# A scan over sixteen states: both channel halves of a state in turn, and five states weighed on another engine

## The chip, the core and the metric

The kernel runs on one core of a Trainium2 chip. A core has five engines with an instruction queue each, worked through in order: TensorE (PE in the profile: matrix products into PSUM, and PEld, its weight loads), VectorE (DVE), ScalarE (ACT), GpSimd (POOL) and SyncE (SP, which here only issues DMA transfers). They wait for each other by semaphores. The metric is the device time of the whole kernel in microseconds; the times shown are those of several executions, and the profile is that of one more.

## What is computed

Four layers over x of shape 2 x 1024 x 128. Each layer normalizes x and adds an attention-like part and a feed-forward part, both of the normalized x. The change lies in layer 2, whose first part is a Mamba block and whose second is a mixture of 14 experts of which each token uses two.

```python
def _L2_attn_ref(x, W_in, conv_w, conv_b, W_x, W_dt, b_dt, A_log, D_param, W_out):
    D_STATE = 16
    D_INNER = 256
    xz = x @ W_in
    xc, z = jnp.split(xz, 2, axis=-1)
    ...
    xc = jax.nn.silu(xc)
    x_dbl = xc @ W_x
    dt_raw = x_dbl[..., :1]
    B_mat = x_dbl[..., 1:1 + D_STATE]
    C_mat = x_dbl[..., 1 + D_STATE:]
    dt = jax.nn.softplus(dt_raw @ W_dt + b_dt)
    A = -jnp.exp(A_log)

    def step(h, inp):
        x_t, dt_t, B_t, C_t = inp
        dA = jnp.exp(dt_t[..., None] * A)
        h = dA * h + dt_t[..., None] * B_t[:, None, :] * x_t[..., None]
        y = jnp.einsum('bds,bs->bd', h, C_t)
        return (h, y)
    ...
    _, ys = lax.scan(step, h0, xs)
    y = jnp.moveaxis(ys, 0, 1) + D_param * xc
    y = y * jax.nn.silu(z)
    return y @ W_out
```

The recurrence runs over 1024 positions for each of 2 batches, 256 channels and 16 states. Every state of a channel is a recurrence of its own; the output of a channel is the sum of its 16 states, each weighed with its row of C.

## The kernel before

`layer2` (L1897) records two generators in turn: `l2_mamba` (L1641), the Mamba block, and the experts (`l2_experts`, `moe_sparse`). Each `yield` of `l2_mamba` hands over; `in_turn` then lets the experts record one piece, at two of three yields up to the 96th yield or so and at every other one behind it. The instructions of both therefore stand interleaved in each engine's queue in the order in which they were recorded, and the loop of the scan lies under `manual_schedule()`, so that nothing is moved afterwards.

The channels lie on the 128 partitions in NH = 2 halves (a), the positions of a batch (b) in two chunks (o) of CH = 512. One scan handles one state s of one half of one chunk: 2 x 2 x 2 x 16 = N = 128 steps k, and `at(k)` (L1767) says which. Before the change the 16 states of one half come first and then the 16 of the other half. What is prepared ahead of the loop: dt and dx = dt * xc for every half, the 16 rows of B written to DRAM (`bd`, L1727) and those of C, split into three bf16 parts, laid into `cst` (L1734).

For each step the loop (L1829 to L1853) records, in this order:

- `inputs(k + 3)` (L1782): GpSimd multiplies dx by the row of B, giving `su`. The row, broadcast to all partitions, was loaded by `load` (L1774) on SP's queue into one of 16 buffers `bb`; the second half uses the rows that the first half loaded.
- `decays(k + 3)` (L1788): ScalarE makes the decays `da` = exp(dt * A) in PSUM, four buffers.
- the `yield`, where a piece of the experts is recorded.
- `scan(k)` (L1794): VectorE's scan over 512 positions, giving `sh`; in the second chunk it starts from `carry`, the last column of the first chunk, which ScalarE copied (L1839).
- the product of step k - 1 (L1843): VectorE weighs `sh` with the row of C, `pc`, giving `spr`. VectorE's order is thus scan k, product k - 1, scan k + 1.
- `rows_c(k)` (L1801): TensorE spreads row s of C over all partitions by a bf16 matmul with a selecting matrix, into the single PSUM bank `pc`, once a step.
- the sum of step k - 1 (L1848): TensorE adds `spr` to the bank `py` by a matmul with the identity (fp32, two passes in the trace), over 16 states.

After 16 states `end` (L1807) adds D * xc on VectorE and multiplies by silu(z) on GpSimd, in place of dx. `project` (L1815) multiplies a finished chunk by W_out, into a bank of `da`; VectorE adds the result to x one step later. PSUM is full: four banks `da`, one `pc`, one `py`, two for the experts.

An expert (`moe_sparse`) records, with a yield between: four transposes m_pt of its rows on TensorE and their copy m_xeT on ScalarE; two products m_ph (two passes each) and their activation m_h on ScalarE, which loads a table for it and another for the next exp; the product m_py and m_yT; four transposes m_pb, the copy m_ye and its store on SP's queue. Its weights m_w and rows m_xe are loaded on SP's queue two experts ahead. When all 14 experts are done, the tokens fetch their rows: GpSimd issues 32 indirect DMAs m_yg (L840); ScalarE and VectorE weigh and add them (m_rows, L857 and L859), TensorE turns four of them back (m_back), and VectorE clips them and adds them to x (m_clip).

The kernel holds all four layers twice: a general branch for inputs that overfill an expert stands behind a flag and doesn't run here.

Of the kernel before, what the change touches and what calls it, by code (L numbers as in the profile page):

```python
# [1640 lines left out]
def l2_mamba(c, w, xnT, xT):  # L1641
# [7 lines left out]
    with ExitStack() as es:  # L1649
# [41 lines left out]
        xc, zs, dt, dx, bd = {}, {}, {}, {}, []  # L1691
        for b in range(B):
# [36 lines left out]
            bd.append(d)  # L1729
            for o in range(0, S, CH):  # L1730
# [27 lines left out]
        bp = es.enter_context(tc.tile_pool(name="s_bp", bufs=16))  # L1758
        wk = es.enter_context(tc.tile_pool(name="s_wk", bufs=3))
        N = 2 * B * NH * L2_DS  # L1760
        carry = {}
# [3 lines left out]
        bb, us, das, hs, pcs, pys = {}, {}, {}, {}, {}, {}  # L1765

        def at(k):  # L1767

            r, s = divmod(k, L2_DS)
            r, a = divmod(r, NH)  # L1770
            b, o = divmod(r, 2)
            return b, o, a, s

        def load(k):  # L1774

            if k < N:
                b, o, a, s = at(k)
                if a == 0:
                    t = bb[2 * b + o, s] = bp.tile([P, CH], F32, tag="bb", name=f"bb{k}")
                    nc.sync.dma_start(t, bd[b][s, o * CH : (o + 1) * CH].partition_broadcast(P))  # L1780

        def inputs(k):  # L1782
            if k < N:
                b, o, a, s = at(k)
                us[k] = wk.tile([P, CH], F32, tag="su", name=f"su{k}")
                nc.gpsimd.tensor_tensor(us[k], dx[b, a][:, o * CH : (o + 1) * CH], bb[2 * b + o, s], ALU.mult)  # L1786

        def decays(k):  # L1788
            if k < N:
                b, o, a, s = at(k)  # L1790
                das[k] = pa.tile([P, CH], F32, tag="da", name=f"da{k}", bufs=4)
                nc.scalar.activation(das[k], dt[b, a][:, o * CH : (o + 1) * CH], AF.Exp, scale=am[:, a, s : s + 1])  # L1792

        def scan(k):  # L1794
            b, o, a, s = at(k)
            hs[k] = wk.tile([P, CH], F32, tag="sh", name=f"sh{k}")
# [4 lines left out]
        def rows_c(k):  # L1801
            if k < N:
                b, o, a, s = at(k)
                pcs[k] = pa.tile([P, CH], F32, tag="pc", name=f"pc{k}")
                mm(c, pcs[k], sel3[:, s, :], cst[b][:, o * CH : (o + 1) * CH])
# [9 lines left out]
        def project(b, o):  # L1815
            po = pa.tile([P, CH], F32, tag="da", name=f"s_po{b}_{o}", bufs=4)
# [3 lines left out]
            return lambda: tt(c, xo, xo, po, ALU.add)  # L1820

        add = None
        with tc.manual_schedule():
            for k in range(L2_DS):
                load(k)
            for k in range(3):
                inputs(k)
                decays(k)
            for k in range(N + 1):  # L1829
                inputs(k + 3)  # L1830
                load(k + 19)
                decays(k + 3)
                if k < N:
                    yield
                    scan(k)
                if k:
                    b, o, a, s = at(k - 1)
                    if o == 0:
# [433 lines left out]
```

## Time and profile before

| what | value |
|---|---|
| three runs | 2029.17, 2033.06, 2038.33 us; median 2033.06 |
| the profiled execution | 2022.65 us, its span 2020.9 |
| busy over the span: PE, DVE, ACT, POOL | 1634.6, 1264.2, 1265.9, 413.6 us |
| the scan loop, 1528 to 1826 us: PE, DVE, ACT, POOL | 234.88, 255.92, 170.25, 202.01 us |
| clock granted to TensorE in these 298 us | 0.89 |
| scan without and with carry, mean | 1217 and 1276 ns, 64 of each |
| da, mean | 690 ns, 128 |

The page of the profile gives the busy time of each engine, the span in 40 slices, the chain of work that ended last, and groups of equal instructions by line and tile with their mean time and the idle time in front of them, put down to what ended it. Where a helper records an operation (`mm` at L51, `tt` at L63), its line is the helper's, and the tile's name tells which it is. Other views give the instructions of a window in order of time, the busy time by window, and who waited for whom. A matmul's duration overlaps its neighbour's, so the distance from start to start is what it costs TensorE.

### The profile page before, as it was taken

How to read it: one execution, taken by the hardware profiler on the slowest of the kernel's cores; microseconds unless marked ns; L12 is line 12 of the kernel's file. 1: busy time of each engine (PE TensorE's matmuls, PEld its weight loads, DVE VectorE, ACT ScalarE, POOL GpSimd, SP SyncE). 2: the span in 40 equal slices, each digit the busy share in tenths (PEclk: the TensorE clock that was granted, in tenths of full speed). 3: DMA queues.
4: the chain of work that ended last, by engine and by line, in shares of the span. 5: the costliest groups of instructions: out<-in, count | busy, mean ns of one | idle time of the engine just before them, and what ended most of it. 6: DMA issues, size and time to landing. Idle time of an engine off the chain costs nothing. (4 is left out here: it accounts for less than half of the span.)

```text
span 2020.9 us, 18408 instructions
## 1 busy us (share of the span) xinstructions
PE 1634.6 (81%) x5978; PEld 730.2 (36%) x5978; DVE 1264.2 (63%) x2130; ACT 1265.9 (63%) x2116; POOL 413.6 (20%) x413
## 2 busy tenths in 40 slices
PE   4699999999688789988888772987785999566784
PEld 2232322222234334433333340654332444223563
DVE  4788866881365446446556338554457998785673
ACT  3378756786477787887877665654556778223451
POOL 2000000000000200000300017033056666761110
PEclk7799989999788899999999885986787999778897
DMA  4521110100100210100100001110014443100000
GB/s 107 161 63 32 25 26 2 25 1 2 48 6 12 62 31 26 31 21 16 38 5 0 8 12 35 58 43 23 9 37 152 136 161 102 42 15 18 6 6 12
DMA packets 76817, 81.66 MB, mean 40 GB/s; under 512 B 12759, under 2 KB 57590, under 8 KB 75560
## 3 DMA queue, kind: packets, MB, share of 16 engines
q1 hardware_dynamic: 67224, 62.68, 10.5%
q0 software_dynamic: 7888, 16.93, 3.4%
q8 instruction: 49, 0.80, 0.2%
q10 hardware_dynamic: 1600, 0.79, 0.2%
q14 instruction: 56, 0.46, 0.1%
HBM read 55.18 MB, written 24.44 MB: 39 GB/s over the span
## 5 line engine op out<-in xcount | busy, mean ns | idle before, releaser
L487 DVE TENSOR_REDUCE maxes<-sc 128x1 f32<-128x1024 f32 x256 | 303.6, 1219 | 79.1 <-PE sc L51 78.3
L602 ACT ACTIVATE ex<-st 128x512 f32<-128x512 f32 x512 | 277.1, 599 | 102.9 <-PE st L51 97.5
L51 PE MATMUL st<-qst,kst 75*128 75x512 bf16 x512 | 178.7, 391 | 8.4 <-DMA qst<-mt 5.6
L51 PE MATMUL sc<-kst,qst 72*128 72x512 bf16 x512 | 161.1, 399 | 28.0 <-DMA kst<-scr 14.1
L1786 POOL TENSOR_TENSOR su<-dx,bb 128x512 f32<-128x512 f32 x128 | 162.3, 1273 | 83.1 <-DVE sh L1797 76.2
L780 POOL DMA_INDIRECT m_x<-m_rows,m_to x80 | 98.6, 1232 | 335.6 <-DVE m_back L742 188.8
L840 POOL DMA_INDIRECT m_yg<-m_y,m_back x80 | 79.8, 998 | 422.9 <-DVE a_y L1045 311.2
L51 PE MATMUL py<-spr,ident 128*128 128x512 f32 x256 | 146.9, 658 | 0.0
L1792 ACT ACTIVATE da<-dt,am 128x512 f32<-128x512 f32 x128 | 87.6, 690 | 83.4 <-DVE sh L1797 79.4
L51 PE MATMUL av<-ex,va 128*9 128x512 f32 x1024 | 139.2, 613 | 0.0
L51 PE MATMUL a_ph<-a_x,wf 128*128 128x512 f32 x256 | 122.6, 614 | 12.7 <-DVE a_x L1046 9.3
L51 PE MATMUL a_pf<-a_h,wf 128*128 128x512 f32 x256 | 114.1, 599 | 0.0
L51 PE MATMUL pc<-cst,sel 80*128 80x512 bf16 x128 | 52.8, 413 | 74.9 <-DVE spr L63 71.0
L51 PEld LDWEIGHTS <-kst 75*128 75x128 bf16 x512 | 49.1, 98 | 168.9 <-issue 126.3
L1007 ACT ACTIVATE a_h<-a_ph,cols 128x512 f32<-128x512 f32 x128 | 84.9, 687 | 33.4 <-PE a_ph L51 33.2
L51 PEld LDWEIGHTS py<-spr,ident 128*128 128x128 f32 x256 | 53.3, 209 | 126.4 <-issue 99.9
L51 PE MATMUL a_pQ<-a_y,wqkvo 128*128 128x512 f32 x56 | 48.0, 1007 | 53.7 <-DVE a_y L1046 53.7
L63 DVE TENSOR_TENSOR spr<-sh,pc 128x512 f32<-128x512 f32 x128 | 85.3, 667 | 8.1 <-PE pc L51 7.9
L63 DVE TENSOR_TENSOR a_r<-a_r,a_x 128x512 f32<-128x512 f32 x32 | 22.0, 690 | 99.1 <-ACT a_r L1018 99.1
L1797 DVE TENSOR_TENSOR_SCAN sh<-da,su 128x512 f32<-128x512 f32 x64 | 77.9, 1217 | 7.5 <-POOL su L1786 4.0
L51 PEld LDWEIGHTS <-qst 72*128 72x128 bf16 x512 | 51.5, 101 | 85.7 <-issue 45.4
L1797 DVE TENSOR_TENSOR_SCAN sh<-da,carry,su 128x512 f32<-128x512 f32 x64 | 81.7, 1276 | 0.2 <-ACT carry L1839 0.2
(541 smaller groups left out, 3224.0 us busy)
## 6 DMA issues: line engine op xcount, KB each, us to landing
bb<-bd SPq DMA_DIRECT2D x64, 256.0 KB
m_w<-in_L_ffn_w_dram SPq DMA_DIRECT2D x44, 128.0 KB
m_xe<-m_x SPq DMA_DIRECT2D x22, 256.0 KB
m_y<-m_ye SPq DMA_DIRECT2D x22, 256.0 KB
qst<-scr POOLq DMA_DIRECT2D x24, 192.0 KB, 9.1
kst<-scr SPq DMA_DIRECT2D x24, 192.0 KB
wf<-in_L_attn_Wf_dram SPq DMA_DIRECT2D x16, 256.0 KB
m_x<-zero SPq DMA_DIRECT2D x1, 3584.0 KB
```

Of the source, the lines that this page charges most:

```text
L51: c.nc.tensor.matmul(out, lhsT, rhs, start=start, stop=stop)
L63: c.nc.vector.tensor_tensor(out, a, b, op)
L487: nc.vector.tensor_reduce(mx[:, t % HT, i : i + 1], sc, AX.X, ALU.max)
L602: nc.scalar.activation(ex, st, AF.Exp)
L780: nc.gpsimd.indirect_dma_start(views[K * t + k][:, :], bass.IndirectOffsetOnAxis(ap=to[:, k, t : t + 1], axis=0), rows[:, t, :], None)
L840: nc.gpsimd.indirect_dma_start(g, None, ys[:, :], bass.IndirectOffsetOnAxis(ap=back[:, k, t : t + 1], axis=0))
L1007: nc.scalar.activation(half(b, f"h{f}", o, "h", f"h{l}_{b}_{f}_{o}", bufs=8), ph, AF.Gelu_apprx_tanh, bias=c.cols["bf1"][:, 4 * l + f : 4 ...
L1786: nc.gpsimd.tensor_tensor(us[k], dx[b, a][:, o * CH : (o + 1) * CH], bb[2 * b + o, s], ALU.mult)
L1792: nc.scalar.activation(das[k], dt[b, a][:, o * CH : (o + 1) * CH], AF.Exp, scale=am[:, a, s : s + 1])
L1797: nc.vector.tensor_tensor_scan(hs[k], das[k], us[k], carry[b, a][:, s : s + 1] if o else 0.0, ALU.mult, ALU.add)
```

## The change

The two halves of a state now follow each other (`at`), so a state is two steps long and both use one load of B and one bank `pc`. Half of the buffers `bb` go; `su` and `sh` get a fourth, `da` drops to three, and each half has a bank `py` of its own. VectorE's product stands right behind its own scan, `decays` and the loads behind the scan. For the states in `APART` the rows of C are loaded from DRAM (`cd`, a new store ahead of the loop) into two buffers `cb`, GpSimd does the product, and its sum is recorded two steps later. `project` uses the bank `pc`, and VectorE's addition follows it at once.

```diff
@@ -1688,7 +1688,7 @@
             for j in range(L2_DC):
                 nc.vector.tensor_scalar(diag[:, a, j, :], c.ident, cw[:, a, j : j + 1], None, ALU.mult)
 
-        xc, zs, dt, dx, bd = {}, {}, {}, {}, []
+        xc, zs, dt, dx, bd, cd = {}, {}, {}, {}, [], []
         for b in range(B):
             xb = xnT[:, b * S : (b + 1) * S]
             for a in range(NH):
@@ -1727,6 +1727,9 @@
             d = dp.tile([L2_DS, S], F32, tag=f"bd{b}", name=f"bd{b}")
             nc.sync.dma_start(d, rows[1 : 1 + L2_DS, :])
             bd.append(d)
+            d = dp.tile([L2_DS, S], F32, tag=f"cd{b}", name=f"cd{b}")
+            nc.sync.dma_start(d, rows[1 + L2_DS :, :])
+            cd.append(d)
             for o in range(0, S, CH):
                 x3 = wk.tile([NR, 3, CH], BF16, tag="x3", name=f"s_x3{b}_{o}", bufs=1)
                 split3(c, wk, rows[:, o : o + CH], x3, f"s_sp{b}_{o}", rtag="u", p=NR)
@@ -1755,54 +1758,82 @@
         prep.close()
 
         pa = es.enter_context(tc.tile_pool(name="s_pa", bufs=1, space=PSUM))
-        bp = es.enter_context(tc.tile_pool(name="s_bp", bufs=16))
+        bp = es.enter_context(tc.tile_pool(name="s_bp", bufs=8))
         wk = es.enter_context(tc.tile_pool(name="s_wk", bufs=3))
         N = 2 * B * NH * L2_DS
+
+        APART = (1, 4, 7, 10, 13)
         carry = {}
         for b in range(B):
             for a in range(NH):
                 carry[b, a] = wp.tile([P, L2_DS], F32, tag=f"carry{b}{a}", name=f"carry{b}{a}")
-        bb, us, das, hs, pcs, pys = {}, {}, {}, {}, {}, {}
+        bb, cb, us, das, hs, pcs, pys = {}, {}, {}, {}, {}, {}, {}
 
         def at(k):
 
-            r, s = divmod(k, L2_DS)
-            r, a = divmod(r, NH)
+            r, a = divmod(k, NH)
+            r, s = divmod(r, L2_DS)
             b, o = divmod(r, 2)
             return b, o, a, s
 
         def load(k):
 
-            if k < N:
+            if k < N and k % NH == 0:
                 b, o, a, s = at(k)
-                if a == 0:
-                    t = bb[2 * b + o, s] = bp.tile([P, CH], F32, tag="bb", name=f"bb{k}")
-                    nc.sync.dma_start(t, bd[b][s, o * CH : (o + 1) * CH].partition_broadcast(P))
+                t = bb[k // NH] = bp.tile([P, CH], F32, tag="bb", name=f"bb{k}")
+                nc.sync.dma_start(t, bd[b][s, o * CH : (o + 1) * CH].partition_broadcast(P))
+
+        apart = [k for k in range(0, N, NH) if at(k)[3] in APART]
+
+        def load_c(n):
+            if n < len(apart):
+                b, o, a, s = at(apart[n])
+                t = cb[apart[n] // NH] = bp.tile([P, CH], F32, tag="cb", name=f"cb{n}", bufs=2)
+                nc.sync.dma_start(t, cd[b][s, o * CH : (o + 1) * CH].partition_broadcast(P))
 
         def inputs(k):
             if k < N:
                 b, o, a, s = at(k)
-                us[k] = wk.tile([P, CH], F32, tag="su", name=f"su{k}")
-                nc.gpsimd.tensor_tensor(us[k], dx[b, a][:, o * CH : (o + 1) * CH], bb[2 * b + o, s], ALU.mult)
+                us[k] = wk.tile([P, CH], F32, tag="su", name=f"su{k}", bufs=4)
+                nc.gpsimd.tensor_tensor(us[k], dx[b, a][:, o * CH : (o + 1) * CH], bb[k // NH], ALU.mult)
 
         def decays(k):
             if k < N:
                 b, o, a, s = at(k)
-                das[k] = pa.tile([P, CH], F32, tag="da", name=f"da{k}", bufs=4)
+                das[k] = pa.tile([P, CH], F32, tag="da", name=f"da{k}", bufs=3)
                 nc.scalar.activation(das[k], dt[b, a][:, o * CH : (o + 1) * CH], AF.Exp, scale=am[:, a, s : s + 1])
 
         def scan(k):
             b, o, a, s = at(k)
-            hs[k] = wk.tile([P, CH], F32, tag="sh", name=f"sh{k}")
+            hs[k] = wk.tile([P, CH], F32, tag="sh", name=f"sh{k}", bufs=4)
             nc.vector.tensor_tensor_scan(
                 hs[k], das[k], us[k], carry[b, a][:, s : s + 1] if o else 0.0, ALU.mult, ALU.add
             )
 
         def rows_c(k):
-            if k < N:
+            if k < N and k % NH == 0 and at(k)[3] not in APART:
                 b, o, a, s = at(k)
-                pcs[k] = pa.tile([P, CH], F32, tag="pc", name=f"pc{k}")
-                mm(c, pcs[k], sel3[:, s, :], cst[b][:, o * CH : (o + 1) * CH])
+                pcs[k // NH] = pa.tile([P, CH], F32, tag="pc", name=f"pc{k}")
+                mm(c, pcs[k // NH], sel3[:, s, :], cst[b][:, o * CH : (o + 1) * CH])
+
+        def weighed(k):
+
+            b, o, a, s = at(k)
+            if s in APART:
+                pr = wk.tile([P, CH], F32, tag="prg", name=f"spr{k}", bufs=2)
+                nc.gpsimd.tensor_tensor(pr, hs[k], cb[k // NH], ALU.mult)
+                if a == NH - 1:
+                    load_c(apart.index(k - a) + 2)
+            else:
+                pr = wk.tile([P, CH], F32, tag="prh", name=f"spr{k}")
+                tt(c, pr, hs[k], pcs[k // NH], ALU.mult)
+            return pr
+
+        def summed(k, pr):
+            b, o, a, s = at(k)
+            if s == 0:
+                pys[b, o, a] = pa.tile([P, CH], F32, tag=f"py{a}", name=f"py{b}_{o}_{a}")
+            mm(c, pys[b, o, a], c.ident, pr, s == 0, s == L2_DS - 1)
 
         def end(b, o, a):
             cs = slice(o * CH, (o + 1) * CH)
@@ -1813,46 +1844,48 @@
             nc.gpsimd.tensor_tensor(y, y, zs[b, a][:, cs], ALU.mult)
 
         def project(b, o):
-            po = pa.tile([P, CH], F32, tag="da", name=f"s_po{b}_{o}", bufs=4)
+            po = pa.tile([P, CH], F32, tag="pc", name=f"s_po{b}_{o}")
             for a in range(NH):
                 mm(c, po, w_out[:, a, :], dx[b, a][:, o * CH : (o + 1) * CH], a == 0, a == NH - 1)
             xo = xT[:, b * S + o * CH : b * S + (o + 1) * CH]
-            return lambda: tt(c, xo, xo, po, ALU.add)
-
-        add = None
+            tt(c, xo, xo, po, ALU.add)
+
+        late = []
         with tc.manual_schedule():
-            for k in range(L2_DS):
+            for k in range(0, 16, NH):
                 load(k)
+            load_c(0)
+            load_c(1)
             for k in range(3):
                 inputs(k)
                 decays(k)
-            for k in range(N + 1):
+            rows_c(0)
+            for k in range(N):
+                b, o, a, s = at(k)
                 inputs(k + 3)
-                load(k + 19)
+                yield
+                scan(k)
                 decays(k + 3)
-                if k < N:
-                    yield
-                    scan(k)
-                if k:
-                    b, o, a, s = at(k - 1)
-                    if o == 0:
-                        nc.scalar.copy(carry[b, a][:, s : s + 1], hs[k - 1][:, CH - 1 : CH])
-                    if s == 0 and k > 1:
-                        end(*at(k - 2)[:3])
-                    pr = wk.tile([P, CH], F32, tag="prh", name=f"spr{k - 1}")
-                    tt(c, pr, hs[k - 1], pcs[k - 1], ALU.mult)
-                rows_c(k)
-                if k:
-                    if s == 0:
-                        pys[b, o, a] = pa.tile([P, CH], F32, tag="py", name=f"py{b}_{o}_{a}")
-                    mm(c, pys[b, o, a], c.ident, pr, s == 0, s == L2_DS - 1)
-                    if add:
-                        add()
-                        add = None
-                    if s == 5 and a == 0 and b + o:
-                        add = project(*divmod(2 * b + o - 1, 2))
-            end(*at(N - 1)[:3])
-            project(1, 1)()
+                if a == NH - 1:
+                    load(k + 15)
+                if o == 0:
+                    nc.scalar.copy(carry[b, a][:, s : s + 1], hs[k][:, CH - 1 : CH])
+                if s == 0 and k > 1:
+                    end(*at(k - NH)[:3])
+                pr = weighed(k)
+                if a == NH - 1:
+                    if s == 4 and k > N // 4:
+                        project(*divmod(2 * b + o - 1, 2))
+                    rows_c(k + 1)
+
+                late.append((k, pr))
+                for n, x in list(late):
+                    if at(n)[3] not in APART or n <= k - 2:
+                        summed(n, x)
+                        late.remove((n, x))
+            for a in range(NH):
+                end(1, 1, a)
+            project(1, 1)
 
 
 def l2_route(c, w, sb, ps, xT):
```

## The prediction

> **What bounds the kernel now.** I read the first page (busy shares, slices, chain of waits), then only the stage that the diff touches: the scan loop of layer 2, whose 128 scans start between 1533.8 and 1822.8 us. The busy time of each engine in stretches of that loop comes first.
>
> ```profile
> core 0: us, PE busy (x) PEld busy (x) DVE busy (x) ACT busy (x) POOL busy (x), PEclk, DMA share, GB/s
> 1600.00:1660.00 60.00, 57.86 (x176) 27.30 (x175) 56.47 (x64) 47.23 (x67) 40.96 (x33) 1.00 0.41 136
> 1714.00:1806.00 92.00, 52.79 (x108) 20.53 (x107) 72.19 (x87) 26.88 (x54) 71.40 (x65) 0.78 0.14 40
> ```
>
> Where the experts of the mixture run beside the scan (first row) TensorE is busy 57.86 of 60 us and VectorE 56.47; GpSimd has a third of its time free. Where the experts are done and their rows are gathered (second row), GpSimd leads with 71.40 of 92, and the clock granted to TensorE falls from 1.00 to 0.78. So the loop has two bounds. I cut it by the starts of scans 0, 10, 90 and 127: 1533.8, 1553.7, 1713.6, 1822.8. That gives a head of 19.9 us, stretch B of 159.9 us (80 steps) and stretch C of 109.3 us.
>
> The timeline of one expert shows what a step of B waits for (start, duration, engine, line, what; in brackets the idle time before it):
>
> ```profile
> 1644.09 0.66 DVE L63 TENSOR_TENSOR spr<-sh,pc 128x512 f32<-128x512 f32 x1
> 1644.11 1.88 PE L51 MATMUL m_ph<-m_xeT,m_w 128*128 128x512 f32 x4
> 1644.67 1.28 DVE L1797 TENSOR_TENSOR_SCAN sh<-da,carry,su 128x512 f32<-128x512 f32 x1
> 1645.83 0.38 PE L51 MATMUL pc<-cst,sel 80*128 80x512 bf16 x1
> 1646.05 1.02 PE L51 MATMUL py<-spr,ident 128*128 128x512 f32 x2
> 1646.24 0.69 DVE L63 TENSOR_TENSOR spr<-sh,pc 128x512 f32<-128x512 f32 x1 [0.29 <-PE pc L51]
> 1646.85 1.28 DVE L1797 TENSOR_TENSOR_SCAN sh<-da,carry,su 128x512 f32<-128x512 f32 x1
> 1648.04 0.66 DVE L63 TENSOR_TENSOR spr<-sh,pc 128x512 f32<-128x512 f32 x1
> ```
>
> Two steps that nothing holds up stand 1.77 us apart (1.19 from the scan to the product, 0.58 from there to the next scan). Here they are 2.18 apart: the row of C (pc) stands in TensorE's queue behind the expert's four passes m_ph, 1.72 us from start to start, and the product spr waits for it. This happens twice an expert, and an expert takes 11.44 us (scans at 1642.90 and 1654.34) for six steps: 6 x 1.77 + 2 x 0.40 = 11.4. TensorE's own sum in it: six sums py at 0.86 (start to start), six rows pc at 0.21, m_ph and m_py at 1.72, two groups of transposes at 0.60: 11.06. TensorE sets the pace of B, VectorE (10.62) stands just behind it, GpSimd (six products su, 7.4) has room.
>
> ```profile
> L1786 POOL TENSOR_TENSOR su<-dx,bb 128x512 f32<-128x512 f32 x128 | 162.3, 1273 | 83.1 <-DVE sh L1797 76.2 <-issue 6.6
> L51 PE MATMUL py<-spr,ident 128*128 128x512 f32 x255 | 146.5, 658 | 0.0
> L63 DVE TENSOR_TENSOR spr<-sh,pc 128x512 f32<-128x512 f32 x128 | 85.3, 667 | 8.1 <-PE pc L51 7.9
> L51 PE MATMUL pc<-cst,sel 80*128 80x512 bf16 x127 | 52.3, 411 | 71.8 <-DVE spr L63 71.0
> L840 POOL DMA_INDIRECT m_yg<-m_y,m_back x32 | 31.2, 976 | 9.1 <-issue 6.8 <-DMA bb<-bd 1.6 <-ACT da L1792 0.3
> ```
>
> These are the stage's groups (count, busy us, mean ns, idle before and its releaser). GpSimd's 83.1 us of idle before su is the room that the change wants to fill. In C it shrinks: from the first gather m_yg (1717.72) to the last su (done 1820.14) are 102.4 us, of which GpSimd waits for scans 18.1 by the view of waits. The waits come in a few holes, like this one:
>
> ```profile
> 1758.95 0.95 POOL L840 DMA_INDIRECT m_yg<-m_y,m_back  x1 [0.30 <-issue]
> 1759.92 1.28 POOL L1786 TENSOR_TENSOR su<-dx,bb 128x512 f32<-128x512 f32 x1
> 1764.93 1.26 POOL L1786 TENSOR_TENSOR su<-dx,bb 128x512 f32<-128x512 f32 x1 [3.73 <-DVE sh L1797]
> ```
>
> Behind the last gather of a group VectorE weighs rows, transposes back and clips before its next scan; GpSimd has run its three steps ahead and stands still.
>
> **The change, part by part.** The built order of both kernels gives the counts (both hold the loop a second time, in a branch that the profile doesn't run): 128 rows pc become 44, VectorE's 128 products become 88, GpSimd gains 40 products, SP 20 loads of 256 KB and two small stores. So it does what it says.
>
> *Stretch B, one period of three states, six steps, one expert.* TensorE loses four of six pc: 11.06 - 4 x 0.21 = 10.2. GpSimd gains two products like su: back to back they start 1.23 apart (1601.19 to 1602.42), and twice it now waits for its own result, 0.1 more by the 0.07 that separates a scan's end from the su it frees: 8 x 1.24 + 0.2 = 10.1. VectorE loses two products, but the order around the others turns: before, scan k stood ahead of product k-1, and the product started 1.19 into a scan of 1.28, before its end. Now product k needs scan k itself. Bounds for that: 1.19 (nothing lost) and 1.5 (0.2 behind the end, the longest wait of a scan on ScalarE's copy); the one dependent pair in the trace, the clip (first instruction 1783.15 + 0.69, second at 1783.88), has 0.04 between them, so I take 1.28 + 0.03 = 1.31. Four full steps of 1.31 + 0.58, and two scans that follow a scan at 1.2 (1.13 to 1.28 by the same rows): 10.0. Half of what the two products gave back is lost again.
>
> The Trainium skill, VectorE: DVE Perf Modes, "The DRAIN you can't avoid", says the opposite: the next instruction starts only when the pipe is empty and a semaphore adds nothing. By it the turned order is free, and VectorE's period 0.5 us shorter; the 1.19 above doesn't fit it.
>
> Three queues at 10.2, 10.1 and 10.0 have no slack between them. Before, the period exceeded its largest queue by 11.44 - 11.06 = 0.38. ScalarE adds something: da has three buffers instead of four and is issued behind scan k, so one step of its lead is gone, and da of the third step stands behind m_yT, which waits for TensorE. Counted from the start of the first full scan, TensorE has its product at 2.0 to 2.4, then py 0.86, m_ph 1.72, pc 0.21, three py 2.58 and m_py 1.72: 9.1 to 9.5. With 0.2 to the handover, m_yT 0.69 and da 0.69 the first scan after the two short ones starts at 10.7 to 11.1 and not at 10.0. I take 10.85, bounds 10.2 and 11.9 (10.2 + 0.38 and 0.65 at both handovers from TensorE to ScalarE, m_h and m_yT). B holds 80/6 = 13.3 periods: 13.3 x (10.85 - 11.44) = **-8 us** (-16 to +6).
>
> *Stretch C.* Twelve of the 40 products stand here: 12 x 1.29 = 15.5. GpSimd's own work before is 34 su x 1.24, 32 gathers x 1.27 (1719.04 to 1720.31) and two products with the gate, 85.3; with the new ones 100.8. Is the idle 18.1 filled? In the new order the gathers of a group's end are followed by two of the new products, then su's whose scans are past: 14 instructions, some 17 us, before the next one that needs the scan behind the clip, against six us of VectorE's work. I take it as filled but for 1.2: 102.0 from first gather to scan 127, against 105.1 (1717.7 to 1822.8): -3. Bounds: -5 and, every hole kept, +12.5. VectorE's instructions with two SBUF operands take longer beside GpSimd's products: m_rows 0.35 beside a gather (1749.15) and 0.87 beside su (1760.49). Twelve more products could do that to twelve of them, 6 us; VectorE isn't C's bound, so I add 1. Together **-2**.
>
> The Trainium skill, SBUF — State Buffer, "Who interferes with whom", gives the rule that speaks against the change: two such instructions exclude each other, the later one fully blocks. That agrees in direction, but 0.87 is less than a whole su of 1.27 added. Were each of C's 20 such instructions (16 m_rows, 4 additions of clipped rows) blocked for a whole su, C would be some 25 us longer (an estimate by that page and the row of su).
>
> *The rest.* Head: 10 loads instead of 16 stand in SP's queue ahead of the experts' first weights; those and m_xe come 3.5 us earlier (16 issues took 9.42), the first transposes had waited 1.1 to 1.9 for m_xe: **-1** (-3 to 0). Projection: VectorE's xT add follows its matmuls at once, where it had a step between and still waited 1.3 to 1.6; behind it stand a scan, and pc of the next state, whose bank it now uses: three times 0.7, **+2** (0 to 5). End: the last two products no longer wait 0.47 for a row (1825.15), both halves' gates follow each other, 1.27 each: **-1** (-1.5 to +1.5). SP's loads of C wait for GpSimd's product two of its states back; behind them stand the stores and weights of experts. These are loaded two experts, 23 us, ahead: nothing, as long as GpSimd lags less than that; without that cover a late m_xe would cost its 1.9 (the wait at the loop's start) an expert. The longer store list ahead of the loop issues at 0.3 us each beside ScalarE's chain: nothing.
>
> Sum: -8 - 2 - 1 + 2 - 1 = **-10 us**. Against the profiled execution (2022.65, span 2020.9, 1.75 around it) that is 2012.6; its time is 10.4 under the median 2033.06, so the median goes to **2023**.
>
> **The rivals.**
> *No time is lost between the queues:* the handovers of ScalarE and TensorE close up, B runs at its largest queue, 10.2 (-16), C at 100.8 (-5), the rest -1: 2011. For it: GpSimd's lead of three steps; against: the 0.38 that was never closed before.
> *TensorE gives it back:* the 0.21 turn into waiting, because sums of GpSimd's products stand in its queue ahead of VectorE's, or a less busy TensorE gets a lower clock: C's 0.78 against B's 1.00 speaks for it (10.2 / 0.9 = 11.3), TensorE's 10.2 of 10.85 against. B +0, C -2, rest 0: 2031.
> *GpSimd held by its own new products (slower):* its queue is in order; if a product arrives before its scan is done, all su behind it wait, and the lead that fills the holes is gone. In B that leaves 11.44 (it waits 0.44 to 0.50 ahead of most su now; 0.17 ahead of each of eight is enough), in C the holes stay, +12.5 + 1; with +0.5 at each of three turns, where two gates of 1.27 now stand together in its queue, and the rest at 0: 2048. It decides when more than 4 of C's 18.1 stay and B gains nothing. For it: 83 us of waits on scans today; against: the su right behind such a product needs the same scan for its buffer, so the wait as such holds up nothing.
>
> **How the numbers follow.** Forecast 0.52, its own range 2015 to 2031; none lost 0.16; given back 0.10; GpSimd held 0.22. The runs shown spread over 9 us, so a measurement can tell about 0.5%, 10 us, from no change. Faster: half of the forecast and the first rival, 0.42. Within: the other half and the second rival, 0.36. Slower: 0.22. The range takes in 2009 to 2049: outside are a third of the first rival and half of the last, 0.16.
>
> **What would show it.** A period of six scans near 10.85 in B with the product 1.31 behind its scan; TensorE still the busiest there at 10.2 of it; GpSimd without holes over 2 us in C; da waiting behind m_yT. Wrong: periods over 11.4, sums waiting for GpSimd's products, or holes in C as before.

## The result and the profile after

The changed kernel takes 2037.31 us in the median (2032.2 to 2044.78) against 2031.88 (2027.04 to 2039.89) of the kernel before on the same chip: a ratio of 1.0024 with a 95% interval of 1.0013 to 1.0035, about 5 us slower. Ten us faster was forecast, with a range of its own of 2015 to 2031 us.

The profiled execution of the changed kernel has a span of 2043.0 us. Scan 0 starts at 1549.02 in it, and at 1533.81 in the one of before; ahead of the loop the change touches only loads and two small stores, and in the kernels below it starts anywhere between 1533.0 and 1549.8. So I compare the loop alone, from scan 0 to scan 127: 289.0 us before, 298.4 after. These 9.4 us are more than the 5.4 between the medians: each is one execution, and that of the changed kernel (2044.78 us) is the slowest of its fifteen, while that of before (2022.65 us) is faster than all fifteen of before. The cuts are those of the prediction, but stretch B is split where a block of 32 steps (one half of the sequence of one batch) ends, at scans 32 and 64.

| us | head, 0 to 10 | block 0, 10 to 32 | block 1, 32 to 64 | block 2, 64 to 90 | C, 90 to 127 | 0 to 127 |
|---|---|---|---|---|---|---|
| before | 19.9 | 42.4 | 64.0 | 53.5 | 109.3 | 289.0 |
| after | 21.8 | 45.1 | 61.1 | 54.1 | 116.4 | 298.4 |

First the busy times of the changed kernel in blocks 0, 1, 2 and stretch C, and in a last line those of C before, with the columns of the prediction's first view (length, then PE, PEld, DVE, ACT, POOL, granted clock, DMA share, GB/s):

```profile
1570.80:1615.85 45.05, 37.58 (x110) 16.55 (x111) 36.15 (x39) 34.66 (x69) 34.55 (x29) 1.00 0.49 145
1615.85:1676.91 61.06, 57.44 (x164) 25.69 (x163) 55.37 (x58) 52.00 (x74) 54.46 (x45) 1.00 0.52 162
1676.91:1730.97 54.06, 48.22 (x137) 21.02 (x135) 43.86 (x48) 42.38 (x81) 44.74 (x37) 1.00 0.39 120
1730.97:1847.38 116.41, 66.06 (x107) 22.92 (x107) 94.57 (x94) 31.21 (x61) 91.47 (x81) 0.68 0.18 57
```

```profile
1713.60:1822.80 109.20, 64.71 (x131) 25.47 (x131) 87.11 (x106) 30.23 (x60) 78.63 (x70) 0.77 0.12 34
```

In block 1 TensorE is busy 94% of the time, as meant. In block 0 no engine is busy more than 84%: there all of them wait for something. In C both VectorE (94.6) and GpSimd (91.5) are busy longer than before (87.1 and 78.6).

What this time in C consists of is told by the groups of VectorE and GpSimd (count, busy us, mean ns of one, idle before and its releaser). The first fence is the kernel before, the second the changed one:

```profile
L859 DVE SCALAR_TENSOR_TENSOR m_rows<-m_yg,r_m,m_rows 128x128 f32<-128x128 f32 x16 | 12.0, 752 | 13.4 <-ACT m_rows L857 7.1 <-DMA m_yg<-m_y,m_back 6.3
L63 DVE TENSOR_TENSOR spr<-sh,pc 128x512 f32<-128x512 f32 x38 | 25.1, 661 | 0.0
L1786 POOL TENSOR_TENSOR su<-dx,bb 128x512 f32<-128x512 f32 x36 | 45.4, 1273 | 19.2 <-DVE sh L1797 19.0
```

```profile
L859 DVE SCALAR_TENSOR_TENSOR m_rows<-m_yg,r_m,m_rows 128x128 f32<-128x128 f32 x16 | 24.7, 1546 | 13.6 <-ACT m_rows L857 8.3 <-DMA m_yg<-m_y,m_back 5.3
L63 DVE TENSOR_TENSOR spr<-sh,pc 128x512 f32<-128x512 f32 x26 | 17.9, 688 | 1.6 <-PE pc L51 0.2
L63 DVE TENSOR_TENSOR m_clip<-xnT,m_back 128x512 f32<-128x512 f32 x4 | 2.7, 687 | 5.2 <-PE m_back L865 5.2
L1798 POOL TENSOR_TENSOR su<-dx,bb 128x512 f32<-128x512 f32 x35 | 43.9, 1267 | 10.4 <-DVE sh L1809 10.3
L1824 POOL TENSOR_TENSOR spr<-sh,cb 128x512 f32<-128x512 f32 x12 | 15.3, 1275 | 3.9 <-issue 2.3 <-PE pc L51 1.5
```

VectorE gave twelve products away (38 at 25.1 us before, 26 at 17.9 now: -7.2) and got +12.7 in sixteen additions m_rows that nobody touched. Busy 94.6 and idle 13.6 + 5.2 + 1.6 + 1.2 (one wait for su) make 116.2 of the 116.4 us; 18.8 us of the waits are for the gathered rows on their way through GpSimd, ScalarE and TensorE (5.3, 8.3 and 5.2). The timeline shows one addition, and GpSimd's queue beside it (start, duration, engine, line, what):

```profile
1759.71 0.95 POOL L840 DMA_INDIRECT m_yg<-m_y,m_back  x1 [0.30 <-issue]
1760.43 5.32 DVE L859 SCALAR_TENSOR_TENSOR m_rows<-m_yg,r_m,m_rows 128x128 f32<-128x128 f32 x1
1760.67 1.28 POOL L1844 TENSOR_TENSOR dx<-dx,zs 128x512 f32<-128x512 f32 x1
1761.89 1.27 POOL L1798 TENSOR_TENSOR su<-dx,bb 128x512 f32<-128x512 f32 x1
1763.11 1.26 POOL L1844 TENSOR_TENSOR dx<-dx,zs 128x512 f32<-128x512 f32 x1
1764.33 1.26 POOL L1798 TENSOR_TENSOR su<-dx,bb 128x512 f32<-128x512 f32 x1
1765.67 2.45 DVE L1809 TENSOR_TENSOR_SCAN sh<-da,carry,su 128x512 f32<-128x512 f32 x2
1765.75 0.99 POOL L840 DMA_INDIRECT m_yg<-m_y,m_back  x1 [0.16 <-issue]
```

m_rows (two operands in SBUF, none in PSUM) takes 0.35 us where nothing disturbs it. Here it begins just ahead of four products of GpSimd that follow each other without a gap, and ends 0.16 us behind the fourth. I call that held: all ten of these additions that took more than 0.6 us ended 0.15 to 0.16 us behind the last of a run of GpSimd's products. The scans, which take da from PSUM, took 1.21 to 1.28 us throughout C, whatever GpSimd did.

In block 0 the wait is another one. The timeline of ScalarE and VectorE over one expert there:

```profile
1590.28 0.70 ACT L1804 ACTIVATE da<-dt,am 128x512 f32<-128x512 f32 x1
1590.82 2.33 DVE L1809 TENSOR_TENSOR_SCAN sh<-da,su 128x512 f32<-128x512 f32 x2
1591.10 1.28 ACT L813 ACT_TABLE_LOAD   x1
1592.39 1.26 ACT L813 ACTIVATE m_h<-m_ph,cols 128x512 f32<-128x512 f32 x2
1593.67 1.28 ACT L1804 ACT_TABLE_LOAD   x1
1594.97 0.69 ACT L1804 ACTIVATE da<-dt,am 128x512 f32<-128x512 f32 x1
1595.60 0.17 ACT L1872 COPY carry<-sh 128x1 f32<-128x1 f32 x1
1595.76 1.22 DVE L1809 TENSOR_TENSOR_SCAN sh<-da,su 128x512 f32<-128x512 f32 x1 [2.62 <-ACT carry L1872]
```

For an expert ScalarE loads a table, makes m_h and loads the other table: 3.9 us without a da. In that time VectorE does the two scans whose products went to GpSimd, one right behind the other; then it has used up the lead and stands still for 2.62 us. (The profile puts this wait down to the copy of the carry, but that copy ends at 1595.77, after the scan began; the da ahead of it ends at 1595.66.) An expert comes back every six steps and so does GpSimd's pair, but a block has 32 steps, five times six and two: from block to block the pair moves by two steps against the expert. Six scans take 12.52 us in block 0 (1583.25 to 1608.28 for twelve), 10.89 in block 1 (1636.43 to 1669.10 for eighteen) and 11.32 in block 2 (1702.06 to 1724.70 for twelve).

### The profile page after: what moved, and what is told of

Read it like the earlier page. It is cut to its first block, busy times and chain, and to the rows that moved or that the text cites. A ratio compares the mean times of both kernels' runs of the same rounds, so it can differ in the third digit from the quotient of the medians.

```text
span 2043.0 us, 18327 instructions
## 1 busy us (share of the span) xinstructions
PE 1636.9 (80%) x5894; PEld 723.0 (35%) x5894; DVE 1258.6 (62%) x2090; ACT 1266.2 (62%) x2116; POOL 458.1 (22%) x453
## 5 line engine op out<-in xcount | busy, mean ns | idle before, releaser
L51 PE MATMUL py<-spr,ident 128*128 128x512 f32 x256 | 153.8, 715 | 67.4 <-DVE spr L63 26.2
L51 PE MATMUL sc<-kst,qst 72*128 72x512 bf16 x512 | 163.2, 404 | 25.7 <-DMA kst<-scr 13.6
L509 POOL DMA_DIRECT2D qst<-mt x16 | 8.6, 537 | 342.3 <-ACT mt L507 342.3
L51 PEld LDWEIGHTS a_ph<-a_x,wf 128*128 128x128 f32 x256 | 49.8, 197 | 77.9 <-issue 56.6
```

Source lines behind the costliest of these rows:

```text
L51: c.nc.tensor.matmul(out, lhsT, rhs, start=start, stop=stop)
L509: (nc.sync, nc.gpsimd, nc.sync)[l].dma_start(qst[s % 3][72 + l : 73 + l, :, h * CH : (h + 1) * CH], mt[l * HG : (l + 1) * HG, :])
```

## The experiments

Theory 1: GpSimd's products lengthen C, either because runs of them hold VectorE's instructions without an operand in PSUM (1a), or by their own length in GpSimd's queue (1b). Theory 2: in B the place of GpSimd's pair against the expert's pieces decides. Theory 3: a product that follows its own scan costs VectorE time that counts. All twelve kernels are timed against the kernel before on their own chip, whose median went from 2023.9 to 2031.4 us with the chip; so the ratios compare, and the stretches come from one profiled execution each.

| us | head | block 0 | block 1 | block 2 | C | 0 to 127 | ratio to before (95%) |
|---|---|---|---|---|---|---|---|
| changed kernel | 21.8 | 45.1 | 61.1 | 54.1 | 116.4 | 298.4 | 1.0024 (1.0013 to 1.0035) |
| 1 order only | 19.2 | 42.6 | 66.2 | 54.6 | 111.7 | 294.3 | 1.0028 (1.0017 to 1.0039) |
| 2 states shifted | 17.5 | 39.4 | 61.0 | 50.3 | 114.8 | 283.0 | 0.9966 (0.9953 to 0.9979) |
| 3 none on GpSimd in C | 18.8 | 45.1 | 61.1 | 54.1 | 115.4 | 294.3 | 1.0019 (1.0007 to 1.003) |
| 4 additions off VectorE | 20.0 | 45.1 | 61.1 | 54.1 | 108.6 | 288.7 | 0.9998 (0.9986 to 1.0009) |
| 5 product a step behind | 19.2 | 40.2 | 59.7 | 53.0 | 114.4 | 286.5 | 0.9988 (0.9975 to 1.0001) |
| 6 = 1 + 4 | 19.2 | 42.6 | 66.2 | 54.6 | 106.6 | 289.1 | 0.9987 (0.9974 to 1.0) |
| 7 = 2 + 4 | 17.5 | 39.4 | 61.0 | 50.3 | 107.6 | 275.8 | 0.9938 (0.9915 to 0.996) |
| 8 = 2 + 4 + 5 | 16.0 | 37.3 | 60.4 | 49.6 | 107.4 | 270.6 | 0.9916 (0.9898 to 0.9935) |
| 9 = 2, block 1 moved | 17.5 | 39.4 | 69.4 | 50.2 | 114.4 | 290.9 | 1.0 (0.9983 to 1.0016) |
| 10 = 8, clip in PSUM | 16.3 | 37.3 | 60.3 | 49.6 | 107.0 | 270.5 | 0.9907 (0.9877 to 0.9937) |
| 11 = 10, one state in C | 16.2 | 37.3 | 60.3 | 49.6 | 101.1 | 264.5 | 0.9875 (0.9849 to 0.9901) |
| 12 = 2 + 5, one state in C | 16.0 | 37.2 | 60.4 | 49.6 | 110.5 | 273.6 | 0.9912 (0.9897 to 0.9926) |

**1. The order alone**, with the change's buffers, and all products on VectorE.

```diff
-        APART = (1, 4, 7, 10, 13)
+        APART = ()
```

> Only the new order of the steps (both halves of a state in turn, one row of C for two steps); all 128 products stay on VectorE. Theory 1 (the order itself costs VectorE, GpSimd's products cost stretch C): every product waits for its own scan, a step is 1.31 + 0.58 = 1.89 instead of 1.77, a period of six scans 11.4 to 11.9, stretch B +0 to +6 us; stretch C as before, 109 to 110 us (scan 90 to 127). In all 0 to +7 us against before, ratio 1.000 to 1.0035. Rival (the order is what stretches C, GpSimd's products are innocent): C 115 to 117 us, ratio 1.003 to 1.006. Rival (fewer rows of C on TensorE alone are worth the 8 us): ratio 0.996.

The periods are 11.6 to 11.7 us, in theory 1's range (a step takes 1.85 to 1.99 us), and the ratio lies in its range; no scan in B waits for a da here. C is 111.7, longer than the 110 allowed. The new order of the steps by itself thus costs about what the whole change costs (1.0028 and 1.0024 can't be told apart); halving TensorE's rows pc brought nothing, since VectorE's queue took over as the longest (busy 62.0 of block 1's 66.2 us, TensorE 60.2). GpSimd's forty products, at the places where they are, earned nothing.

**2. GpSimd's states shifted by block**, so that its pair is at steps 4 and 5 of every six in all blocks with experts; block 2 then has four such states, not five. The same expression replaces the test for APART wherever it stands.

```diff
-        APART = (1, 4, 7, 10, 13)
+        APART = ((2, 5, 8, 11, 14), (1, 4, 7, 10, 13), (3, 6, 9, 12), (1, 4, 7, 10, 13))
+
+        def is_apart(k):
+            b, o, a, s = at(k)
+            return s in APART[2 * b + o]
```

> The states that GpSimd weighs are shifted in blocks of 32 steps 0 and 2, so that they stand at the same place of an expert's period as in block 1. Theory 2 (blocks 0 and 2 lose because ScalarE's three or four pieces for an expert stand just at the two short scans, and da comes late): periods of six scans fall from 12.5 to about 10.9 in block 0 and from 11.4 to about 10.9 in block 2, stretch B 151 to 154 us instead of 160.2, the whole 6 to 9 us faster than the changed kernel: ratio to before 0.998 to 0.9995. Rival (block 0 is slow for the weights or the first loads of the experts, not for the place of the pieces): block 0 stays at 12 or more, ratio 1.0015 to 1.003.

Theory 2 holds: block 0 now runs at 10.91 (1560.60 to 1593.32 for eighteen), block 2 at 10.67 (1687.06 to 1708.39 for twelve). B takes 150.7 us; the prediction's 8 us off 159.9 would have been 151.9. By the ratios the gain over the changed kernel is 11.8 us (0.9966), more than expected; in the profile 9.5 of it are B's, and the head is shorter too. The timeline of the same pieces of ScalarE in block 0:

```profile
1588.65 1.28 ACT L813 ACT_TABLE_LOAD   x1
1589.14 1.22 DVE L1814 TENSOR_TENSOR_SCAN sh<-da,su 128x512 f32<-128x512 f32 x1
1589.95 1.26 ACT L813 ACTIVATE m_h<-m_ph,cols 128x512 f32<-128x512 f32 x2
1591.13 1.22 DVE L1814 TENSOR_TENSOR_SCAN sh<-da,su 128x512 f32<-128x512 f32 x1
1591.23 1.28 ACT L1809 ACT_TABLE_LOAD   x1
1592.53 0.69 ACT L1809 ACTIVATE da<-dt,am 128x512 f32<-128x512 f32 x1
```

They are as long as before, but lie beside full steps: VectorE spends two da in 4.2 us (1589.14 to 1593.32) instead of 2.3, and the lead suffices.

**3. No products on GpSimd from step 90.**

```diff
+            return s in APART and k < 90
```

> GpSimd weighs its states only up to step 90; in the stretch of the gathers VectorE weighs all. Theory 1 (GpSimd's products cost stretch C, by holding VectorE's additions of two SBUF rows or by their own 15.5 us): stretch C (scan 90 to 127) falls from 116.4 to 107 to 110 us, the 16 additions m_rows from 24.7 back to 12 to 14 us in all, the whole 6 to 9 us faster than the changed kernel, ratio 0.998 to 0.9995. Rival (C is longer for the order of the steps, or for TensorE's clock of 0.68): C stays at 114 or more, ratio 1.002 to 1.003.

Theory 1 misses: C is 115.4, not 107 to 110, and the rival's "114 or more" holds. Its groups on VectorE:

```profile
L63 DVE TENSOR_TENSOR spr<-sh,pc 128x512 f32<-128x512 f32 x38 | 26.1, 688 | 2.3
L859 DVE SCALAR_TENSOR_TENSOR m_rows<-m_yg,r_m,m_rows 128x128 f32<-128x128 f32 x16 | 11.0, 686 | 9.4 <-ACT m_rows L857 5.0 <-DMA m_yg<-m_y,m_back 4.4
L63 DVE TENSOR_TENSOR m_clip<-xnT,m_back 128x512 f32<-128x512 f32 x4 | 2.7, 687 | 8.6 <-PE m_back L865 8.6
```

The hold is gone (24.7 to 11.0, so GpSimd's products were its cause), but VectorE has its twelve products back (+8.2), and it waits longer for TensorE (m_back 8.6 against 5.2, the projection 3.9 against 0.0). So in C the products on GpSimd win and lose about the same. The waits for TensorE are not a matter of this edit alone: from step 90 on kernel 1 has the same instructions, waits 8.3 us for TensorE where this one waits 12.5, and needs 111.7. The granted clock was 0.79 there and 0.73 here. These 3.7 us are a warning for every comparison of C below: a difference of that size between two single executions needn't come from the edit. (Blocks 0, 1 and 2 repeat within 0.1 us where the instructions are the same.)

**4. The addition off VectorE.** ScalarE weighs the second gathered row as it does the first, and TensorE adds both rows while it transposes them.

```diff
+                elif name == "m2":
+                    if t % 4 == 0:
+                        rows2 = sb.tile([P, 4, D], F32, tag="rows2", name=f"{name}_rows2_{t}", bufs=2)
+                    nc.scalar.activation(rows2[:, t % 4, :], got[t][k], AF.Identity, scale=gate)
...
-                    nc.tensor.transpose(pt[:, j * P : (j + 1) * P], rows[:, t - 3 + j, :], c.ident)
+                    if name == "m2":
+                        mm(c, pt[:, j * P : (j + 1) * P], rows[:, t - 3 + j, :], c.ident, True, False)
+                        mm(c, pt[:, j * P : (j + 1) * P], rows2[:, j, :], c.ident, False, True)
...
```

> As the changed kernel, but in layer 2 the addition of the two gathered and gated rows is taken off VectorE: ScalarE writes the second row times its gate, and TensorE adds both while it transposes back. Theory 1a (VectorE's additions with two SBUF operands are held by runs of GpSimd's products, and what follows them is late): stretch C falls from 116.4 to 107 to 111 us, VectorE's busy time there by 20 us or more, ratio 0.998 to 1.000. Theory 1b (GpSimd's own queue, longer by 15.5 us, sets C): C stays within 2 us of 116.4, since 100.8 us of GpSimd's work stands there in either kernel; ratio 1.0015 to 1.003.

C falls by 7.8 us, VectorE's work in it by 20.9, as theory 1a said; 1b alone is refuted, since GpSimd's work is the same. So VectorE's work was a bound of C. The view of C:

```profile
1724.50:1833.10 108.60, 62.70 (x155) 26.95 (x155) 73.69 (x79) 36.02 (x77) 91.23 (x81) 0.75 0.20 61
```

Now GpSimd's 91.2 is the largest by far, and VectorE waits 14.1 us for su, where it had waited 1.2, and 13.9 us for m_back, where it had waited 5.2.

**5. VectorE's product a step behind its scan again.**

```diff
-                pr = weighed(k)
...
+                if s in APART:
+                    late.append((k, weighed(k)))
+                if k and at(k - 1)[3] not in APART:
+                    late.append((k - 1, weighed(k - 1)))
```

> The changed kernel, but VectorE's product stands one step behind its scan again (scan k, then the product of step k-1), as before the change. Theory 3 (the product that needs the scan just ahead of it costs VectorE 0.12 to 0.15 us a step, and VectorE's queue is part of the chain that sets stretch C): 37 steps of C lose it, C falls from 116.4 to 110 to 113 us, a lone step from 1.92 to 1.77 us, the whole 4 to 8 us faster than the changed kernel, ratio to before 0.9985 to 1.0005. Rival (as predicted: VectorE bounds neither B nor C, so its order is free): C within 1.5 us of 116.4, ratio 1.0015 to 1.0035.

Half a hit: 7 us are won, and a lone step (one that nothing holds up, with a carry) is 1.77 us instead of 1.92 to 1.98, so the order isn't free. But C lost only 2.0 us; its additions are still held (20.4 us). Most came from block 0, 45.1 to 40.2 (its period fell to 11.30, 1580.24 to 1602.84 for twelve); why the late da costs less in this order stays open. Theory 3 is right on the price of a step and wrong on the place where it counts.

**6. Kernel 1 with the edit of kernel 4.** It asks what that edit is worth where GpSimd weighs nothing.

> No products on GpSimd (all 128 on VectorE, new order of steps), and the addition of two gathered rows off VectorE as in the run before. It tells what that edit is worth without GpSimd's new products. Theory 1a (there the edit won 7.8 us of C because runs of GpSimd's products held the additions for 24.7 us): with 11.1 us of additions it wins less than half of that, C 108 to 111 us against 111.7, ratio 1.001 to 1.0025. Rival (any 10 us less of VectorE's work in C would have done the same, products of GpSimd or not): C 101 to 105 us, ratio 0.998 to 1.000.

C is 106.6, won 5.1: between the two. The ratio, 0.9987, lies in the rival's range and not in theory 1a's: by the ratios the edit wins 0.0041 here and 0.0026 in kernel 4, by the profile 5.1 and 7.8 us. With 3.7 us between kernels 1 and 3, these can't be told apart. So taking work off VectorE shortens C with or without GpSimd's new products, and how much of C's loss is the hold that they add is not shown.

**7 and 8. The edits together.** (In 8 the projection of block 1 stands one state earlier, where its bank is free.)

> Both edits together: GpSimd's states shifted by block, and the addition of two rows off VectorE. Theories 1a and 2 (two separate losses, one in B, one in C): the gains add, 13.7 and 6.8 us off the changed kernel, about 2017 us, ratio 0.993 to 0.995; stretch B near 151, C 107 to 109 us. Rival (they share a cause, or the end of B hands its gain to C): ratio 0.9955 to 0.9975.

> The two edits and VectorE's product one step behind its scan. Theory 3: another 2 to 5 us less than with the two edits alone, ratio 0.991 to 0.993, lone steps of 1.77 us. Rival (with the additions gone from VectorE, GpSimd's 91 us and TensorE set the pace, and VectorE's order is free): as with the two edits alone, 0.993 to 0.995.

Both hit. 7: the gains of 2 and 4 add (0.0058 and 0.0026 off 1.0024 make 0.9940), so the two edits mend two separate losses. 8: 4.9 us less from scan 0 to scan 90, and none in C.

**9. Kernel 2 with the pair of block 1 at the bad place.** Block 1 then has four such states, not five.

```diff
-        APART = ((2, 5, 8, 11, 14), (1, 4, 7, 10, 13), (3, 6, 9, 12), (1, 4, 7, 10, 13))
+        APART = ((2, 5, 8, 11, 14), (3, 6, 9, 12), (3, 6, 9, 12), (1, 4, 7, 10, 13))
```

> As the kernel with GpSimd's states shifted by block, but block 1 (steps 32 to 63), which was good in either, now has GpSimd's pair where block 0 of the changed kernel had it (steps 2 and 3 of every six). Block 1 copies no carry on ScalarE. Theory 2a (the place alone decides: ScalarE's pieces for an expert stand at the two short scans): the periods of block 1 rise from 10.9 to 12 to 12.6 us, the block from 61.0 to 64 to 67 us. Theory 2b (it takes the place and the copies of the carry together, as in blocks 0 and 2): periods stay under 11.5 us, the block under 63.

The period of block 1 is 12.54 (1632.45 to 1644.99), that of block 0 in the changed kernel; the block takes 69.4, more than expected. So the place is enough to bring the loss about, with no carry copied. VectorE's waits for da inside block 1, of this kernel and then of kernel 2 (total, times, longest):

```profile
DVE sh L1814 <- ACT da L1809: 6.8, 3, 2.3
```

```profile
DVE sh L1814 <- ACT da L1809: 1.9, 3, 0.6
```

**10 and 11. The clip.** In kernel 8 another instruction without an operand in PSUM is held instead, the clip. In 10 its three steps work in the bank m_back:

```diff
-        tt(c, t, xn[:, cs], acc, ALU.add)
-        nc.vector.tensor_scalar(t, t, -100.0, 100.0, ALU.max, ALU.min)
-        tt(c, x[:, cs], x[:, cs], t, ALU.add)
+        tt(c, acc, xn[:, cs], acc, ALU.add)
+        nc.vector.tensor_scalar(acc, acc, -100.0, 100.0, ALU.max, ALU.min)
+        tt(c, x[:, cs], x[:, cs], acc, ALU.add)
```

> As the kernel with states shifted, additions off VectorE and the product one step behind its scan, but the clip of a group's rows stays in PSUM (three instructions on VectorE with an operand in PSUM each, where the middle one had both in SBUF and took 2.3 us in the mean instead of 0.43). Theory 1a (any instruction of VectorE with no operand in PSUM is held by GpSimd's products): the four clips take 2 to 3 us in all instead of 9.2, C falls from 107.3 to 100 to 104 us, ratio 0.988 to 0.9905. Rival (GpSimd's 91.5 us and the way through TensorE set C now): C within 2 us of 107.3, ratio 0.991 to 0.9925.

In 11 GpSimd weighs one state instead of five in the last block:

```diff
-        APART = ((2, 5, 8, 11, 14), (1, 4, 7, 10, 13), (3, 6, 9, 12), (1, 4, 7, 10, 13))
+        APART = ((2, 5, 8, 11, 14), (1, 4, 7, 10, 13), (3, 6, 9, 12), (4,))
```

> As the run before, but in the last block GpSimd weighs one state instead of five (VectorE weighs the others). With no operand of VectorE held any more, theory 1a expects GpSimd's products in C to be no loss, so VectorE's eight more products at 0.66 cost: C 0 to 3 us longer than in the run before. Rival (GpSimd's queue sets C now, 91.5 us busy of 107): C 2 to 6 us shorter, ratio 0.987 to 0.990.

The clip of kernel 8, then of kernel 10:

```profile
L1935 DVE TENSOR_SCALAR m_clip<-m_clip 128x512 f32<-128x512 f32 x4 | 9.2, 2300 | 0.1
```

```profile
L1934 DVE TENSOR_SCALAR m_back<-m_back 128x512 f32<-128x512 f32 x4 | 2.8, 699 | 0.1
```

The hold is gone, 6.4 us of VectorE's time, and C doesn't move (107.4 to 107.0): the rival, though the ratio, 0.9907 (0.9877 to 0.9937), can't tell the two apart. In 11 eight products return to VectorE and C falls by 5.8: the rival again. C of kernel 10 and of kernel 11:

```profile
1705.20:1812.20 107.00, 67.23 (x157) 28.03 (x156) 70.04 (x80) 36.23 (x78) 91.67 (x81) 0.76 0.21 62
```

```profile
1702.00:1803.10 101.10, 63.77 (x161) 27.70 (x160) 74.03 (x87) 36.45 (x78) 81.98 (x73) 0.81 0.19 55
```

GpSimd's 91.67 of 107 became 81.98 of 101.1: once nothing holds VectorE, C follows GpSimd's queue, and taking eight products out of it is worth more than VectorE pays for them. Kernel 11 is the fastest, 2001.66 us, ratio 0.9875.

**12. Schedule alone**: shifted states, one state in the last block, the product a step behind; additions and clip untouched.

> The changed kernel with nothing but another schedule of its products: GpSimd's states shifted by block, one state instead of five for it in the last block, VectorE's product one step behind its scan. The additions of two rows and the clip stay on VectorE as they were. Theory 1a (the additions are held only by runs of GpSimd's products, which C no longer has): the 16 additions take 11 to 13 us, C 107 to 111 us, head and B as in the other kernels with both edits (1542 to 1705: 163 us from scan 0 to scan 90), ratio 0.991 to 0.994. Rival (the moves of rows and clip off VectorE's two SBUF operands are not needed once GpSimd has room): C 100 to 103 us, ratio 0.986 to 0.989.

All of theory 1a's numbers hold (additions 12.6 us, C 110.5, 163.1 us from scan 0 to scan 90, 0.9912). There are two ways to free C: fewer products on GpSimd (from kernel 5's 114.4 to 110.5), and nothing on VectorE that they can hold (to 107.0 in kernel 10). Together, in kernel 11, they make 101.1, near their sum (103.1).

## Why the prediction was wrong

**Stretch B, -8: +0.3.** The step that failed is "B holds 80/6 = 13.3 periods: 13.3 x (10.85 - 11.44)". The period itself was right, 10.89 where it was walked, and so was its mechanism: the scan behind the two short ones waits 0.63 us for a da that stands behind m_yT (it starts at 1647.32), and the product stands 1.31 behind its scan, 0.60 ahead of the next:

```profile
1647.32 1.28 DVE L1809 TENSOR_TENSOR_SCAN sh<-da,carry,su 128x512 f32<-128x512 f32 x1 [0.63 <-ACT da L1804]
1649.31 1.28 DVE L1809 TENSOR_TENSOR_SCAN sh<-da,carry,su 128x512 f32<-128x512 f32 x1
1650.62 0.69 DVE L63 TENSOR_TENSOR spr<-sh,pc 128x512 f32<-128x512 f32 x1
1651.22 1.28 DVE L1809 TENSOR_TENSOR_SCAN sh<-da,carry,su 128x512 f32<-128x512 f32 x1
```

But it was walked for one place of the pair against the expert and multiplied over three. Block 1 gained 2.9 us, block 0 lost 2.6, block 2 lost 0.6. The lead of da that shrank to three buffers was named in the prediction and charged only at m_yT; at the other places the table loads, 3.9 us with m_h, meet it. Kernel 2 and kernel 9 switch this on and off.

**Stretch C, -2: +7.1 in the profiled executions.** Two steps failed. The first is "I take it as filled but for 1.2". GpSimd's work grew by 12.8 us (78.63 to 91.47; the new products took 15.3, where 15.5 was counted), but its idle time shrank by 5.6 only. Waits for scans of 10.3 us are left ahead of su in place of 19.0, and 3.8 us have come ahead of three of its new products, which start 0.13 to 0.14 us behind the end of a scan. The second is "VectorE isn't C's bound, so I add 1". Before, VectorE was busy 87.1 and waited 21.9 of 109.2 us; after, it was busy 94.6. The additions alone took 12.7 us more, not 1; and kernel 4, with 20.9 us less of VectorE's work and all of GpSimd's, is 7.8 us shorter in C. So VectorE's queue was a part of the chain, and a late VectorE is what left GpSimd's holes open.

What the 7.1 us consist of stays open. Kernel 3 frees the additions and leaves C at 115.4, since VectorE has its products back; kernel 1, with the same instructions there, has 111.7; kernel 5 wins 2.0 with the old order. The three causes, the hold, the turned order and GpSimd's longer queue, are each seen, but single executions don't price them. The lower clock (0.77 to 0.68) doesn't show as longer waits of VectorE for TensorE: these were 8.4 us before and 5.4 after.

The Trainium skill, SBUF — State Buffer, "Who interferes with whom", was set aside because one addition had lasted 0.87, less than a whole su:

```profile
1760.49 0.87 DVE L859 SCALAR_TENSOR_TENSOR m_rows<-m_yg,r_m,m_rows 128x128 f32<-128x128 f32 x1 [1.08 <-ACT m_rows L857]
```

That row was misread: the su beside it had begun 0.57 us earlier, at 1759.92, so only 0.71 us of it were left, and the addition ended 0.16 us behind its end, like the held ones after the change. And it was an argument from one instruction: over all sixteen the time above 0.35 each was 6.4 us before and 19.1 after. With the page's rule at full weight, +25, C would have been over-forecast; its sign was right. Two bounds of C don't come out of their own terms either: with no hole left C would be 100.8 - 105.1 = -4.3, with every hole kept 100.8 + 18.1 - 105.1 = +13.8.

**The order.** The Trainium skill, VectorE: DVE Perf Modes, "The DRAIN you can't avoid", was read in the prediction as making the turned order free. The section goes on: "A next op that is not held starts earlier" (held in a sense of its own), which fits the product that starts 1.19 us into a scan of 1.28. Kernel 5 shows that the turned order costs 0.15 to 0.21 us a lone step (1.77 against 1.92 to 1.98), where 0.12 was taken; and in kernel 1 the new order outweighs TensorE's 64 spared rows pc.

**Small terms.** End -1: -1.0 (7.54 to 6.53 us from scan 127 to the last projection's addition). Projection +2: the waits for s_po rose from 6.7 to 8.8. Head -1: kernels 3 and 4, which have the changed kernel's head, give 18.8 and 20.0 where it gives 21.8 and before 19.9: no size can be told.

**The rivals.** The slower one had the sign and the holes left in C, but not the mechanism: GpSimd does wait ahead of its new products, 0.6 to 0.7 us once a period in B, yet as much in block 1 at 10.89 us as in block 0 at 12.52, and 3.8 us in all of C. "TensorE gives it back" named the clock, and in C it did fall; kernels 1 and 3 differ by 3.7 us there with the same instructions, and what of it is the clock's is not settled.

## What to carry to other kernels

Where two rhythms meet (an expert every six steps, blocks of 32), walk the period at every place that the one can have against the other, before multiplying. Where two engines wait for each other in turn, neither has room: add each queue's work and waits, and count a new microsecond on either of them. Before work goes to GpSimd, list VectorE's instructions that have no operand in PSUM beside it: they pay for whole runs of its products.

## What the hardware showed

- An instruction of VectorE with all operands in SBUF isn't held for one instruction of GpSimd but for a run: 5.32 us instead of 0.35 through four products, until GpSimd came to a gather. An in-place clip of 128x512 took 2.30 us in the mean of kernel 8 instead of 0.43; with its operand in PSUM, 0.70 in kernels 10 and 11, with GpSimd's products beside it or without. Scans with da in PSUM took 1.19 to 1.28 in the loops of all kernels.
- Removing one held instruction leaves the hold to the next of its kind: the four clips took 1.7 us in the changed kernel, 4.8 in kernel 4 without the additions, and 9.2 in kernel 8.
- A load of ScalarE's table took 1.28 us, and the activation started right behind it (1591.10, 1592.39).
- In C of the changed kernel the clock granted to TensorE went between 0.50 and 1.00 from one 8 us window to the next, and so it did before the change.
